# Turning the attention weights by DMA instead of on TensorE in a graph-network kernel

## The chip, the cores and the metric

The kernel runs on one core of one Trainium2 chip. The metric is the time of one execution on the device in microseconds (us); lower is better. A kernel's time is the median over its runs. One execution with a hardware profile stands beside the times.

Five engines work side by side, each on its own list of instructions in a fixed order: TensorE (PE in the profile; PEld is its loading of weights), VectorE (DVE), ScalarE (ACT), GpSimd (POOL) and SyncE (SP), which here only issues DMA transfers. They wait for each other through semaphores. TensorE writes to PSUM; the kernel uses eight banks of 128 x 512 fp32 numbers.

## The reference, cut to what matters

There are 128 graphs of 128 nodes with 256 features; `x` is 128 x 128 x 256 fp32, `adj` a 0/1 matrix for each graph.

```python
# layer 0: three rounds of a gated graph network
h = relu(layernorm(x))
A = (adj != 0)
for i in range(3):
    m = h @ weight[i]
    aggr = einsum('bst,bsd->btd', A, m)           # sum over the edges that come in
    h = gru_cell(aggr, h, w_ih, w_hh, b_ih, b_hh) # gates r, z, n
x = x + h
# layer 1: one graph-attention layer
h = relu(layernorm(x))
Wh = h @ W
s = Wh.sum(-1)
e = leaky_relu(s[:, :, None] + s[:, None, :], 0.2)
e = where(adj == 0, -inf, e)
alpha = softmax(e)                                # over the last axis
x = x + einsum('bpq,bqo->bpo', alpha, Wh)
```

The change concerns the last two lines: the exponentials of `e` (128 x 128 for a graph) are needed with rows and columns exchanged before TensorE can multiply them with `h`.

## The kernel before, in words

**Tiling.** Four graphs make a group (`G = 4`), so there are `NG = 32` groups. A group passes through three rounds of the GRU and then the attention. One round of one group is a *turn*; the list `turns` in the kernel interleaves the 96 turns so that three groups are in flight.

**A turn.** The products of the GRU are arranged as a fast matrix scheme of seven block products (function `products`). They use six PSUM banks: `x_rz`, `x_n`, `y_rz`, `y_n`, `q_rz`, `q_n`. In their order they are X1, Q5, Y6, Y7, X2, Y4, Q3 (the letter is the bank, the number the block product; in the last round, which works on rows, five and seven, three and four are exchanged). Between Y6 and Y7, and between Y7 and Y4, ScalarE copies `y_rz` and `y_n` to SBUF (`put`, L691), and TensorE may not write the bank again before that copy has read it.

**Attention of a group** (function `attention`). The steps are: `normed` writes `h1` (there is one such buffer); VectorE forms the node scores `s`; TensorE spreads `s` over a bank (L891); VectorE adds, applies the leaky relu and takes the row maximum (L885 to L904); ScalarE takes the exponential (L909), with a change of function table before and after; VectorE sums it (L911); TensorE turns the four 128 x 128 tiles of `e` into a bank `misc` (L917); ScalarE copies the bank to `eT` (L919, one buffer); TensorE multiplies `h1` by `eT` in two pieces (`weighted`, L610) and ScalarE copies each to `uT`; TensorE multiplies `uT` by `W` (L930, two pieces); VectorE scales by the inverse sum and adds to `x1` (L935); SyncE stores. The last group does this in two halves.

**The filler banks.** All products on TensorE that are not of the GRU scheme, the edge sums (L596) and the four kinds of attention (L891, L917, L610, L930), take turns in two PSUM banks, both called `misc`.

**DMA transposes that exist already.** Where `h` changes between rows and columns, `turned_halves` (L535 to L539) splits each fp32 number into its two 16-bit halves, which ScalarE writes as two planes (`pl`), turns both planes with one DMA transpose issued by SyncE (L545), and lets ScalarE put the halves together again. One such step covers 128 x 512 numbers, as many as the attention weights of a group.

**What sets the order.** Nothing runs in the order of the source text. Every operation is recorded with an engine, a cost in ns that the author gave, its reads and writes, and a due time (class `Plan`). `Plan.run` then simulates the engines with these costs, and at each step issues on each engine, among the operations that could start first, the one with the most urgent rank. A rank comes from the due time of the operation and of all that depends on it. The GRU products are a fixed chain with due times of one `SLOT` for each turn; what feeds the chain must be ready `MARGIN` ns ahead of it. `plan.due` gives the due time of a group's attention, in slots. The result is a static order for each engine; the costs have no other effect on the program.

Of the kernel before, what the change touches and what calls it, by code (L numbers as in the profile page):

```python
# [16 lines left out]
P = 128  # L17
G = 4
# [2 lines left out]
SETS = 4  # L21
EARLY = 3
SLOT = 18150
MARGIN = 5000
GATES = 18150
BIG = 3.0e38

# [9 lines left out]
class Plan:  # L37
# [28 lines left out]
    def op(self, eng, ns, fn, reads=(), writes=(), room=(), due=None, mark=None,  # L66
           turn=None, two=False, lag=None):

        i, deps = len(self.nodes), set()
        for b in room:
            if b.prev is not None:
                deps.update(a[0] for a in b.prev.accesses)
        for is_write, group in ((False, reads), (True, writes)):
            for item in group:
                b, lo, hi = item if isinstance(item, tuple) else (item, 0, 1 << 30)
                for j, w, l, h in b.accesses:
                    if (w or is_write) and l < hi and lo < h:  # L80
                        deps.add(j)
                if is_write and b.prev is not None:
                    deps.update(a[0] for a in b.prev.accesses)
        for is_write, group in ((False, reads), (True, writes)):
            for item in group:
                b, lo, hi = item if isinstance(item, tuple) else (item, 0, 1 << 30)
                b.accesses.append((i, is_write, lo, hi))
        deps.discard(i)
        bufs = {id(x[0] if isinstance(x, tuple) else x): (x[0] if isinstance(x, tuple) else x)
                for x in list(reads) + list(writes) + list(room)}  # L90
        free = [b for b in bufs.values() if self.tags[b.tag][1] in ("free", "turn")]
        for b in free:
            b.users.append(i)
            b.left += 1
        self.nodes.append([eng, ns, fn, deps, free, self.due if due is None else due,
                           two or eng == "POOL", self.LAG[eng] if lag is None else lag])
        if due is not None:
            self.chain.append(i)
        if mark is not None:
            self.marks[mark] = i  # L100
        if turn is not None:
            self.turns.append((i, turn))
# [108 lines left out]
def kernel(  # L211
# [37 lines left out]
        "at": (1, "all", work, [P, G, N]), "a": (6, "all", work, [P, G, N]),  # L249
        "hT": (1, "set", work, [P, KD, GN]), "rows": (3, "turn", work, [P, G, D]),  # L250
        "pl": (1, "turn", work, [P, 2, 3, GN]), "plT": (1, "turn", work, [P, 2, 3, GN]),
        "r1": (1, "turn", work, [P, G, D]), "p3": (1, "turn", work, [P, G, D]),
        "hs": (2, "turn", work, [P, 4, H]), "aT": (2, "turn", work, [P, KD, GN]),
        "gs": (2, "turn", work, [P, 4, H]),
# [21 lines left out]
        "w1": (1, "all", const, [P, KD, D]), "w1_out": (1, "all", const, [P, KD]),  # L276
        "w1_sum": (1, "all", const, [P, D]),
    }
    DTYPE = {"at": I32, "a": BF16, "pl": U16, "plT": U16, "p3": BF16}
    phys = {}  # L280

    def make(tag, n, kind, pool, shape):
# [191 lines left out]
    def normed(src, dst, lo=0, hi=G):  # L474

        st, mv, rs, nm = buf("st"), buf("mv"), buf("rs"), buf("nm")
        part = slice(lo, hi)
        for b in range(lo, hi):
            op("DVE", 415, lambda b=b: nc.vector.bn_stats(ap(st)[:, b, :], ap(src)[:, b, :]),
               [(src, b, b + 1)], [(st, b, b + 1)])  # L480

        def aggr():
            for b in range(lo, hi):
                nc.vector.bn_aggr(ap(mv)[:, b, :], ap(st)[:, b, :])
        op("DVE", 160 * (hi - lo), aggr, [st], [mv])

        def rstd():
            nc.gpsimd.tensor_tensor(ap(rs)[:, part], ap(mv)[:, part, 1], eps[:, part], OP.add)
            nc.gpsimd.tensor_tensor(ap(rs)[:, part], ap(rs)[:, part], neghalf[:, part], OP.pow)
        op("POOL", 1300, rstd, [mv], [rs])  # L490
        op("DVE", 170, lambda: nc.vector.scalar_tensor_tensor(
            ap(nm)[:, part], ap(mv)[:, part, 0], -1.0, ap(rs)[:, part], op0=OP.mult, op1=OP.mult),
           [mv, rs], [nm])
        for b in range(lo, hi):
            op("ACT", 600, lambda b=b: nc.scalar.activation(
                ap(dst)[:, b, :], ap(src)[:, b, :], AF.Relu, bias=ap(nm)[:, b:b + 1],
                scale=ap(rs)[:, b:b + 1]), [(src, b, b + 1), rs, nm], [(dst, b, b + 1)])

    def flat(b):
        return ap(b).rearrange("p q n -> p (q n)")  # L500
# [26 lines left out]
    def turned_halves(src, rows, dst):  # L527

        pl, plT = buf("pl"), buf("plT")

        def planes(b, k):
            return ap(b)[:, k, 0:2].rearrange("p two (g m) -> p two g m", g=G)
        for k in range(KD):
            units = [src] if rows else [(src, 2 * k, 2 * k + 2)]
            op("ACT", 960, lambda k=k: nc.scalar.copy(  # L535
                planes(pl, k), halves_of(src, rows)[:, k]), units, [(pl, k, k + 1)])
            transpose(pl, plT, k, 2)
            units = [(dst, 2 * k, 2 * k + 2)] if rows else [dst]
            op("ACT", 960, lambda k=k: nc.scalar.copy(  # L539
                halves_of(dst, not rows)[:, k], planes(plT, k)),  # L540
               [(plT, k, k + 1)], units)

# [272 lines left out]
    def phase(g, layer):  # L815
        return turns.index((g, layer))

    def group(g):
        graphs = slice(g * G, (g + 1) * G)
        plan.phase = phase(g, 0)  # L820
        plan.due = (plan.phase - 1) * SLOT
        rows0, at, a, hT = buf("rows"), buf("at"), buf("a"), buf("hT")
        op("SP", 100, lambda: nc.sync.dma_start(ap(rows0), x[graphs].rearrange("b n d -> n b d")),
           [], [rows0])
        op("SP", 100, lambda: nc.sync.dma_start(ap(at), adj[graphs].rearrange("b n m -> n b m")),
           [], [at])
        op("DVE", 420, lambda: nc.vector.tensor_scalar(ap(a), ap(at), 0.0, None,
                                                       op0=OP.not_equal), [at], [a])
        plan.due = (phase(g, L - 1) + 2) * SLOT
        normed(rows0, rows0)  # L830
        for layer in range(L):
            plan.phase = phase(g, layer)
            if layer == 0:
                if g < EARLY:
                    rows_to_T(rows0, hT)
                else:
                    turned_halves(rows0, True, hT)
                parts = parts_of(rows0)
            elif layer < L - 1:
                parts = turned_parts(hT)  # L840
            else:
                rows, x1, h1 = buf("rows"), buf("x1"), buf("h1")
                turned_halves(hT, False, rows)
                parts = parts_of(rows)
                op("SP", 100, lambda: nc.sync.dma_start(
                    ap(x1), x[graphs].rearrange("b n d -> n b d")), [], [x1])
            hs, aT, gs = buf("hs"), buf("aT"), buf("gs")
            node_sums(hT, hs, "POOL", 1390, 940)
            edge_sums(parts, a, aT)
            node_sums(aT, gs, "DVE", 690, 440)  # L850
            plan.cursor = plan.phase * SLOT
            if layer < L - 1:
                gru(layer, hT, hs, aT, gs)
        plan.due = (phase(g, L - 1) + 3) * SLOT
        gru_rows(L - 1, hT, hs, aT, gs, rows, x1)
        for lo, hi in ((0, G),) if g < NG - 1 else ((G // 2, G), (0, G // 2)):
            attention(g, a, x1, h1, lo, hi)

    def attention(g, a, x1, h1, lo, hi):
# [47 lines left out]
        def exps():  # L907
            for b in range(lo, hi):
                nc.scalar.activation(ap(e)[:, b, :], ap(e)[:, b, :], AF.Exp, bias=ap(low)[:, b:b + 1])  # L909
        op("ACT", 2600 + 390 * n, exps, [low], [e], turn=(g + 2, 1, "rz"))  # L910
        op("DVE", cost, lambda: nc.vector.tensor_reduce(small(den), es(), AX.X, OP.add), [e], [den])  # L911
        op("DVE", 170, lambda: nc.vector.reciprocal(small(rden), small(den)), [den], [rden])
        p_e, eT, uT = buf("misc"), buf("eT"), buf("uT")

        def turn():
            for b in range(lo, hi):
                nc.tensor.transpose(flat(p_e)[:, b * N:(b + 1) * N], ap(e)[:, b, :], ident)  # L917
        op("PE", 110 * n, turn, [e], [p_e], [eT])
        op("ACT", 190 + 100 * n, lambda: nc.scalar.copy(  # L919
            ap(eT)[:, part].rearrange("p b n -> p (b n)"), flat(p_e)[:, lo * N:hi * N]),  # L920
           [p_e], [(eT, lo, hi)])

        weighted(h1, eT, uT, lo, hi)
        for m in range(lo, hi, 2):
# [13 lines left out]
        op("SP", 100, lambda: nc.sync.dma_start(  # L938
            out[g * G + lo:g * G + hi].rearrange("b n d -> n b d"), ap(x1)[:, part]),
           [(x1, lo, hi)], [])  # L940

    weights()
    for g in range(NG):
# [33 lines left out]
```

## Time and profile before

| | |
|---|---|
| time, median of 3 runs | 2150.49 us (2149.06 to 2151.18) |
| span of the profiled execution | 2151.8 us |
| PE busy | 2124.3 us, 99% |
| PEld busy | 1894.7 us, 88% |
| DVE busy | 1693.9 us, 79% |
| ACT busy | 1543.7 us, 72% |
| POOL busy | 948.4 us, 44% |
| 16 DMA engines, mean share | 24.9% over three queues |
| DMA transposes | 186, median 3.3 us from issue to landing |

Busy time is the union of an engine's instructions. [...] the cost of a matmul in a stream is the distance from one start to the next, not its duration. In the timeline, neighbouring instructions of one line are merged; "x4" is their number, and an fp32 matmul shows as two records, except the transposes, which show as one.

### The profile page before, as it was taken

To read this page: it belongs to the slowest core of one execution; us is meant where nothing else is said; L and a number is where in the kernel's file an instruction comes from. 1 tells how busy PE (TensorE), PEld (TensorE's weight loads), DVE (VectorE), ACT (ScalarE), POOL (GpSimd) and SP (SyncE) were. 2 spreads that over 40 slices of the span, in tenths; PEclk is the share of its full clock that TensorE was granted. 3 is DMA by queue.
4 is the path that set the end of the run, shared out by engine and by line. 5 is a ranking of instruction groups with operands and counts; after the bars stand their busy time and mean duration, and the time that the engine had idled before them with its cause. 6 is when DMAs were issued, how large, how long until landed. Compare 5 with 4: busy or idle time off the path is not lost.

```text
span 2151.8 us, 34116 instructions
## 1 busy us (share of the span) xinstructions
PE 2124.3 (99%) x12670; PEld 1894.7 (88%) x12670; DVE 1693.9 (79%) x3297; ACT 1543.7 (72%) x2675; POOL 948.4 (44%) x889
## 2 busy tenths in 40 slices
PE   8999999999999999999999999999999999999997
PEld 7888888998889998888998899998899988898885
DVE  5778887887877778777787877878777787877776
ACT  5567877776777777767777777777777778676673
POOL 5645453344544435443445534445534345334331
PEclk9999999999999999999999999999999999999998
DMA  4222122222322222212122223223222213212110
GB/s 142 45 50 50 43 43 64 59 50 50 70 62 57 60 50 50 69 50 69 42 52 65 67 52 62 48 53 66 62 57 60 50 45 69 74 36 49 40 50 30
DMA packets 301750, 121.49 MB, mean 56 GB/s; under 512 B 232976, under 2 KB 301328, under 8 KB 301584
## 3 DMA queue, kind: packets, MB, share of 16 engines
q1 hardware_dynamic: 301584, 119.31, 24.5%
q8 instruction: 99, 1.62, 0.3%
q14 instruction: 67, 0.55, 0.1%
HBM read 45.36 MB, written 16.78 MB: 29 GB/s over the span
## 4 chain that ended last, share of the span: by engine, by line
PE 92%; DVE 5%; DMA 1%; ACT 1%; issue 1%; POOL 0%; DVEq 0%; ACTq 0%; POOLq 0%
PE y_rz L654 14%; PE q_rz L654 10%; PE x_rz L654 10%; PE y_rz L661 8%; PE y_n L654 7%; PE misc L596 6%; PE q_rz L661 5%; PE x_rz L661 5%; PE x_n L654 5%; PE q_n L654 5%; PE misc L930 5%; PE y_n L661 4%; PE x_n L661 3%; PE misc L610 3%; PE q_n L661 3%
## 5 line engine op out<-in xcount | busy, mean ns | idle before, releaser
L624 POOL TENSOR_TENSOR hs<-hT 128x512 f32<-128x512 f32 x96 | 128.8, 1342 | 326.3 <-PE y_n L661 275.9
L556 POOL TENSOR_TENSOR r<-rows 128x512 f32<-128x512 f32 x128 | 146.5, 1163 | 259.8 <-ACT rows L539 170.9
L691 ACT COPY t_rz<-y_rz 128x512 f32<-128x512 f32 x192 | 112.0, 583 | 191.9 <-PE y_rz L654 111.1
L654 PE MATMUL y_rz<-hs,s_hh 128*128 128x256 f32 x768 | 198.6, 381 | 0.2 <-ACT t_rz L691 0.2
L654 PE MATMUL y_rz<-gs,s_x 128*128 128x256 f32 x768 | 197.4, 380 | 0.0
L694 DVE TENSOR_TENSOR t_rz<-t_rz,q_rz 128x512 f32<-128x512 f32 x192 | 131.1, 683 | 70.0 <-ACT t_rz L691 36.5
L654 PEld LDWEIGHTS y_rz<-gs,s_x 128*128 128x128 f32 x768 | 146.4, 191 | 20.0
L654 PEld LDWEIGHTS y_rz<-hs,s_hh 128*128 128x128 f32 x768 | 144.3, 191 | 21.2 <-ACT t_rz L691 1.8
L628 POOL TENSOR_TENSOR hs<-hT,hs 128x256 f32<-128x256 f32 x96 | 75.0, 789 | 196.2 <-PE q_n L661 186.1
L559 POOL TENSOR_TENSOR p<-r 128x512 bf16<-128x512 f32 x128 | 155.5, 1233 | 0.3
L798 POOL TENSOR_TENSOR x<-x,u 128x512 f32<-128x512 f32 x64 | 84.8, 1341 | 157.9 <-DMA x<-in_x_dram 83.6
L691 ACT COPY t_n<-y_n 128x512 f32<-128x512 f32 x192 | 112.4, 585 | 52.3 <-PE y_n L654 20.7
L694 DVE TENSOR_TENSOR t_n<-t_n,q_n 128x512 f32<-128x512 f32 x192 | 131.1, 683 | 23.8 <-ACT t_n L691 9.1
L599 ACT COPY aT<-misc 128x512 f32<-128x512 f32 x192 | 111.7, 584 | 38.0 <-PE misc L596 30.3
L654 PE MATMUL x_rz<-aT,s_x 128*128 128x256 f32 x512 | 131.5, 379 | 0.0
L654 PE MATMUL x_rz<-hT,s_hh 128*128 128x256 f32 x512 | 131.5, 379 | 0.0
L576 POOL TENSOR_TENSOR d<-hT,pl 128x512 f32<-128x512 f32 x64 | 84.1, 1318 | 93.9 <-ACT pl L574 84.1
L930 PE MATMUL misc<-w,uT 128*128 128x256 f32 x512 | 122.8, 384 | 0.3 <-ACT uT L615 0.2
L755 ACT ACTIVATE u<-u,bias_i 128x512 f32<-128x512 f32 x128 | 92.1, 721 | 37.8 <-DVE u L746 37.5
L654 PE MATMUL y_n<-hs,s_hh 128*128 128x256 f32 x384 | 114.5, 380 | 0.3 <-ACT t_n L691 0.2
L654 PE MATMUL y_n<-gs,s_x 128*128 128x256 f32 x384 | 114.3, 379 | 0.0
L763 DVE TENSOR_TENSOR hT<-u,d 128x512 f32<-128x512 f32 x128 | 110.1, 862 | 3.5
(212 smaller groups left out, 6425.7 us busy)
## 6 DMA issues: line engine op xcount, KB each, us to landing
rows<-in_x_dram SPq DMA_DIRECT2D x32, 512.0 KB, 4.3
x<-in_x_dram SPq DMA_DIRECT2D x32, 512.0 KB, 3.9
out_dram<-x SPq DMA_DIRECT2D x31, 512.0 KB, 2.9
at<-in_adj_dram SPq DMA_DIRECT2D x32, 256.0 KB, 2.9
plT<-pl SPq DMA_TRANSPOSE x186, 3.3
rz<-in_L_gnn_w_ih_dram SPq DMA_DIRECT2D x1, 768.0 KB, 5.0
e<-in_L_gnn_weight_dram SPq DMA_DIRECT2D x3, 256.0 KB, 5.6
rz<-in_L_gnn_w_hh_dram SPq DMA_DIRECT2D x1, 768.0 KB, 7.9
```

The costliest lines, as they stand in the source:

```text
L556: op("POOL", 1106, lambda part=part: nc.gpsimd.tensor_tensor(ap(r1)[:, part], ap(rows)[:, part], top(rows)[:, part], OP.subtract), [(rows, ...
L559: op("POOL", 1050, lambda part=part: nc.gpsimd.tensor_tensor(ap(p3)[:, part], ap(r1)[:, part], top(r1)[:, part], OP.subtract), [(r1, n, n ...
L596: nc.tensor.matmul(flat(ps)[:, b * N:(b + 1) * N], part(i, b, k), ap(a)[:, b, :], start=(i == 0), stop=(i == 2))
L599: op("ACT", 590, lambda k=k, ps=ps: nc.scalar.copy(ap(dst)[:, k, :], flat(ps)), [ps], [(dst, 2 * k, 2 * k + 2)])
L624: op(eng, cost, lambda: sub(ap(w)[:, 0:2, :], blocks()[:, 1::2, :], blocks()[:, 0:2, :], OP.subtract), [t], [(w, 0, 2)], two=True)
L654: nc.tensor.matmul(ap(bank)[:, half, :], ap(w)[:, i - 1, q, :], source(t, sums), start=(first and c == 0 and m == 0), stop=False, skip_gro ...
L661: nc.tensor.matmul(ap(bank)[:, m, half * P:(half + len(chunk)) * P], source(t, sums)[:, m * N:(m + 1) * N], ap(w)[:, i - 1, q:q + len(chun ...
L691: op("ACT", 590, lambda: nc.scalar.copy(ap(t), ap(y)), [y], [t])
L694: op("DVE", 690, lambda: nc.vector.tensor_tensor(ap(t), ap(t), ap(q), OP.add), [q], [t])
L755: op("ACT", 723, lambda j=j, cols=cols: nc.scalar.activation(ap(u)[:, cols], ap(u)[:, cols], AF.Tanh, bias=ap(W["bias_i"])[:, 2 * KD + j:2 ...
L763: op("DVE", 690, lambda j=j, d=d, cols=cols: nc.vector.tensor_tensor(ap(hT)[:, j, :], ap(u)[:, cols], ap(d), OP.add), [(u, lo, hi), d], [( ...
L930: nc.tensor.matmul(ap(ps)[:, b, :], ap(uT)[:, k, (m + b) * N:(m + b + 1) * N], ap(w1)[:, k, :], start=(k == 0), stop=(k == KD - 1))
```

## The change

The four transposes on TensorE, and the copy from their bank, are replaced for 30 of the 32 groups. ScalarE now splits `e` into 16-bit halves (`pe`), one DMA transpose turns both planes (`peT`), and ScalarE interleaves the halves again into `eT`. This frees TensorE of the transposes and frees the `misc` bank they used. The last two groups keep the old way. The scheduler gets a larger `MARGIN`, other costs for several ScalarE operations, and a due time for the attention of the last groups that is no later than half a slot after the last turn.

```diff
-MARGIN = 5000
+MARGIN = 8000
...
+        "pe": (1, "all", work, [P, 2, G * N]), "peT": (1, "all", work, [P, 2, G * N]),
...
-            op("ACT", 600, lambda b=b: nc.scalar.activation(
+            op("ACT", 520, lambda b=b: nc.scalar.activation(
...
-            op("ACT", 960, lambda k=k: nc.scalar.copy(
+            op("ACT", 1045, lambda k=k: nc.scalar.copy(
                 planes(pl, k), halves_of(src, rows)[:, k]), units, [(pl, k, k + 1)])
...
-            op("ACT", 960, lambda k=k: nc.scalar.copy(
+            op("ACT", 1340, lambda k=k: nc.scalar.copy(
                 halves_of(dst, not rows)[:, k], planes(plT, k)),
...
-        plan.due = (phase(g, L - 1) + 3) * SLOT
+        plan.due = min(phase(g, L - 1) + 3, len(turns) + 0.5) * SLOT
...
-        op("ACT", 2600 + 390 * n, exps, [low], [e], turn=(g + 2, 1, "rz"))
+        op("ACT", 2570 * (g < NG - 1) + 320 * n, exps, [low], [e], turn=(g + 2, 1, "rz"))
...
-        p_e, eT, uT = buf("misc"), buf("eT"), buf("uT")
-
-        def turn():
-            for b in range(lo, hi):
-                nc.tensor.transpose(flat(p_e)[:, b * N:(b + 1) * N], ap(e)[:, b, :], ident)
-        op("PE", 110 * n, turn, [e], [p_e], [eT])
-        op("ACT", 190 + 100 * n, lambda: nc.scalar.copy(
-            ap(eT)[:, part].rearrange("p b n -> p (b n)"), flat(p_e)[:, lo * N:hi * N]),
-           [p_e], [(eT, lo, hi)])
+        eT, uT = buf("eT"), buf("uT")
+        if g < NG - 2:
+            turned_weights(e, eT)
+        else:
+            p_e = buf("misc")
...
...
+    def turned_weights(e, eT):
+        pe, peT = buf("pe"), buf("peT")
+        def halves(t):
+            return ap(t).rearrange("p g n -> p (g n)").bitcast(U16).rearrange(
+                "p (m two) -> p two m", two=2)
+        op("ACT", 1045, lambda: nc.scalar.copy(ap(pe), halves(e)), [e], [pe])
+        op("SP", 100, lambda: nc.sync.dma_start_transpose(
+            ap(peT).rearrange("p two (g q) -> p (two g) q", q=P),
+            ap(pe).rearrange("p two m -> p (two m)")), [pe], [peT])
+        op("ACT", 1340, lambda: nc.scalar.copy(halves(eT), ap(peT)), [peT], [eT])
```

More of the change, by code (lines that the diff above doesn't have):

```diff
@@ L278 @@
     }
-    DTYPE = {"at": I32, "a": BF16, "pl": U16, "plT": U16, "p3": BF16}
+    DTYPE = {"at": I32, "a": BF16, "pl": U16, "plT": U16, "pe": U16, "peT": U16, "p3": BF16}
     phys = {}
@@ L909, in exps, with turn @@
                 nc.scalar.activation(ap(e)[:, b, :], ap(e)[:, b, :], AF.Exp, bias=ap(low)[:, b:b + 1])
-        op("ACT", 2600 + 390 * n, exps, [low], [e], turn=(g + 2, 1, "rz"))
+        op("ACT", 2570 * (g < NG - 1) + 320 * n, exps, [low], [e], turn=(g + 2, 1, "rz"))
         op("DVE", cost, lambda: nc.vector.tensor_reduce(small(den), es(), AX.X, OP.add), [e], [den])
         op("DVE", 170, lambda: nc.vector.reciprocal(small(rden), small(den)), [den], [rden])
-        p_e, eT, uT = buf("misc"), buf("eT"), buf("uT")
-        def turn():
-            for b in range(lo, hi):
-                nc.tensor.transpose(flat(p_e)[:, b * N:(b + 1) * N], ap(e)[:, b, :], ident)
-        op("PE", 110 * n, turn, [e], [p_e], [eT])
-        op("ACT", 190 + 100 * n, lambda: nc.scalar.copy(
-            ap(eT)[:, part].rearrange("p b n -> p (b n)"), flat(p_e)[:, lo * N:hi * N]),
-           [p_e], [(eT, lo, hi)])
+        eT, uT = buf("eT"), buf("uT")
[3 more added lines that the diff above has]
+            p_e = buf("misc")
+            def turn():
+                for b in range(lo, hi):
+                    nc.tensor.transpose(flat(p_e)[:, b * N:(b + 1) * N], ap(e)[:, b, :], ident)
+            op("PE", 110 * n, turn, [e], [p_e], [eT])
+            op("ACT", 190 + 100 * n, lambda: nc.scalar.copy(
+                ap(eT)[:, part].rearrange("p b n -> p (b n)"), flat(p_e)[:, lo * N:hi * N]),
+               [p_e], [(eT, lo, hi)])
         weighted(h1, eT, uT, lo, hi)
```

## The prediction

> **What bounds the kernel now.** I read the page's busy shares and slices first, then the waits of TensorE, then its timeline in a middle stretch and at the end.
>
> ```profile
> PE 2124.3 (99%) x12670; PEld 1894.7 (88%) x12670; DVE 1693.9 (79%) x3297; ACT 1543.7 (72%) x2675; POOL 948.4 (44%) x889
> PE   8999999999999999999999999999999999999997
> PEclk9999999999999999999999999999999999999998
> ```
>
> TensorE is full in every slice but the first and the last. Busy could still hide stretched matmuls, so I checked the waits from 110 to 2000 us (first three lines) and 2000 to 2112 us (last two):
>
> ```profile
> PE misc L610 <- ACT aT L599: 2.6, 2, 1.6
> PE y_n L654 <- ACT t_n L691: 0.2, 1, 0.2
> PE y_rz L654 <- ACT t_rz L691: 0.2, 1, 0.2
> PE q_rz L661 <- DVE gs L624: 1.8, 1, 1.8
> PE misc L610 <- ACT eT L919: 0.4, 1, 0.4
> ```
>
> That is 5.2 us of waiting in 2000 us. So in the middle any work taken off TensorE is time taken off the kernel, and any work added on another engine is free until TensorE waits for it. The removed transposes stand in this stream:
>
> ```profile
> 1025.93 0.59 PE L654 MATMUL y_n<-gs,s_x 128*128 128x256 f32 x2
> 1026.37 0.60 PE L917 MATMUL misc<-ident,e 128*128 128x128 f32 x4
> 1026.80 1.03 PE L654 MATMUL y_rz<-hs,s_hh 128*128 128x256 f32 x4
> ```
>
> The columns are start, length, and instruction. The four transposes last 0.60 us, but from their start to the next start is 0.43 us; that is their price. They stand between Y6 (ends with y_n) and Y7 (starts with y_rz). The end is different:
>
> ```profile
> 2109.57 3.62 PE L930 MATMUL misc<-w,uT 128*128 128x256 f32 x16
> 2115.64 0.72 PE L891 MATMUL misc<-ident,s 128*128 128x128 f32 x3
> 2116.59 0.32 PE L891 MATMUL misc<-ident,s 128*128 128x128 f32 x1 [0.22 <-DVE hw L867]
> 2121.12 1.35 PE L917 MATMUL misc<-ident,e 128*128 128x128 f32 x4 [4.21 <-ACT e L909]
> ```
>
> The last GRU product has been issued at 2115.64 us. From there to the end, 36.2 us, the attention of the last two groups runs with TensorE waiting, and the chain of waits names VectorE for most of 2117 to 2136 us. The L930 products at 2109.57 us stood ahead of that point, on the full engine.
>
> **What the Trainium skill says.** *VectorE: DVE Perf Modes*, "The three transpose paths", gives a 128x128 bf16 transpose 390 ns on TensorE (into PSUM) and 1309 ns by DMA (into SBUF). In the stream here four fp32 ones cost 0.43 us, so 108 ns each; the DMA ones land 3.3 us after issue. The DMA way is slower, then, and pays only because TensorE is the full engine. *DMA: Bandwidth & Descriptors*, "DMA Transpose (X-bar)", admits 2-byte types only, which is why ScalarE must split and join; the existing copies around such transposes measure 1046 and 1338 ns. *ScalarE: Activation LUTs*, "What ACT_TABLE_LOAD costs", gives 1283 ns for a load; the trace has 31 before the exponentials, mean 1283 ns. *TensorE: Matmul & The Clock Gate*, part 1, says an idle array drops to half clock for some microseconds. The trace agrees: after 2120 us the clock is 0.66 to 0.78 and L930 starts lie 0.43 us apart, against 0.22 us before.
>
> **The change part by part.**
>
> *Removed from TensorE.* 30 groups x 0.43 us (timeline above; the spread is small, all have one form) = 12.9 to 13.1 us. I take **13.1**, four times 109.5 ns a group.
>
> *ScalarE.* Added per group: one split of 1.05 us and one join of 1.34 us, the same 128x1024 16-bit forms as L535 and L539. Removed: the copy from the bank, 0.59 us. 30 x (1.05 + 1.34 - 0.59) = 54 us, so 1544 becomes about 1598 us, 75% of a span of 2136. It lies beside the full TensorE: **0**, as long as no copy of Y (L691) comes late behind a 1.34 us join.
>
> *DMA.* 30 transposes join 186, of the same size, each some 1.3 us of SyncE's issue time; the DMA engines go from 25% to perhaps 28%. The chain from exponential to L610 grows from about 1 us (transposes, copy) to 1.05 + 3.3 + 1.34 plus hand-overs, some 6.5 us. Behind the waiting DMA on SyncE stand loads for later turns and other transposes; behind the waiting join on ScalarE stand copies of Y, for which TensorE does wait. The bounds come from the landings of the transposes in the trace, 3.0 to 5.4 us. The plan prices the new one at 4.1 us (100 ns and the usual lag of 4000). The 122 joins that exist waited 0.2 us in all for their DMA. In the new program's order 25 us or more of TensorE work lie between L891 of a group and its first L610 (51 to 56 us before), for score additions 3, exponential with tables 4 to 5, and the 6.5: enough. I take **1 us** lost over the 30 groups; bounds 0 and 8 (a quarter of a microsecond each, if half of the late landings reach ScalarE at a bad moment).
>
> *Fillers.* Between Y6 and Y7 TensorE has to give ScalarE time for the copy. In the old order 5 of 96 such places had nothing between, in the new one 8; 49 have an L610 piece and 27 an L930 piece where L917 or L891 stood. In the trace of before the empty places cost 0.2 us each at most. **0**, bounds 0 and 2.
>
> *New costs and margin.* They change no instruction. They bring the plan to the durations in the trace: 520 for the relu (2.07 us for four), 1045 and 1340, 2570 for two tables and 320 an exponential (1.28 us for four). The named waits of 4.9 us in mid-kernel may go or come elsewhere: **0**, bounds -3 and +3.
>
> *Start.* The new order loads `x` and `w_hh` ahead of the first message weight (which landed at 6.45 us; the fourth transfer landed at 10.24). The first composed weights come later, but what ended TensorE's start was VectorE's gs at 28.6 us (a wait of 3.4 us). Walking the new VectorE order with the old durations, gs comes at about 27, and four small transposes already stand inside the wait. **1 us gained**, bounds -2 and +3.
>
> *End.* With the common due time both L930 pieces of group 29 move behind the last GRU product: one ahead of L891 of group 30, one after it. Counting the order with the start-to-start prices, work up to the last product falls from 2082.1 to 2065.5 us: 16.6 = 13.1 + 3.5. The 3.5 us move into the wait of 4.2 us. It isn't all gain. L891 comes 1.7 us after the last product instead of at once, so the score chain (3.1 us on VectorE) starts about 0.9 us later; the four L935 of group 29 (0.42 us each) now stand in the VectorE chain ahead of the next normalisation, partly under GpSimd's 1.0 us there; and L917 of group 30 must wait for its bank until the first L935 pair has read it. I make the tail 1.5 to 2.5 us longer: **1.5 gained** net, bounds -1 and +3.5.
>
> Sum: 13.1 - 1 + 0 + 0 + 1 + 1.5 = 14.6; 2150.5 - 14.6 = **2136 us**.
>
> **The rivals.**
>
> *A. The DMA becomes a wait on ScalarE.* Landing at 5.4 instead of 3.3 us leaves ScalarE standing for about 1.5 us, and copies of Y behind it come late; 0.25 us for each of 30 groups on TensorE is 7.5 us: 2143.5. For: ScalarE's order is static and goes to 75%. Against: 122 such joins wait 0.2 us in all now.
>
> *B. Start and end give their full bound.* 13.1 + 3.5 + 3 = 19.6: 2131. For: VectorE was late with L935 and hw just before the last products, and gets free there. Against: the VectorE chain of the end is only reordered.
>
> *C. Slower.* If every transpose is late by its whole spread (2.1 us), and half reaches TensorE, 30 x 1.05 = 31 us against 14.6 gained: 2167; with 0.6 us each, 2154. For: one `eT`, one `pe`, one `h1`, so a late group holds up the next one's scores. Against: 25 us less 3, 4.5 and 6.5 leaves some 11 us of slack in that chain.
>
> *D. No change*, 2150: the filler places left bare cost as much as the transposes did, 0.44 us at each of 30. Against: at the places that are bare now, 0.2 us at most.
>
> **How the numbers follow.** Forecast 0.71, A 0.12, B 0.09, C 0.05, D 0.03. Predicted is 2136. B lies at the lower edge and A at the upper one: 2130.5 to 2143 leaves out C, D and the outer parts of A and B, about 0.17 in all. Faster by over 0.2% (under 2146.2) takes in the forecast, A and B, 0.92; same 0.03; slower 0.05.
>
> **What would show each step.** TensorE busy falls by some 13 us with 120 fewer matmuls; L917 is left with 8 of 128. The waits of TensorE between 110 and 2090 us stay under 8 us, none on L610 from the new join. ScalarE's joins wait for DMA a few us in all; rival A shows there as 20 us and more, with Y products waiting for L691. The last GRU product comes about 16 to 18 us earlier than 2115.6, with L930 right behind it; the tail after it is 37 to 39 us. The first gs product comes near 27 us. The forecast is wrong if TensorE's summed waits grow by more than 7 us, or the tail by more than 5.

## The result and the profile after

The changed kernel takes 2140.14 us (median of 6 runs, 2138.75 to 2141.19) against 2150.78 us (6 runs, 2148.45 to 2151.4). The ratio is 0.9952, 95% interval 0.9939 to 0.9965: 10.3 us less, between 7.5 and 13.1. The forecast of 2136 was 4 us too low; the time lies in the stated range.

The page of the changed kernel, its busy line and TensorE's slices:

```profile
PE 2108.1 (99%) x12550; PEld 1879.9 (88%) x12550; DVE 1750.7 (82%) x3297; ACT 1587.1 (74%) x2705; POOL 951.0 (45%) x889
...
PE   8999999999999999999999999999999999999997
```

TensorE runs 120 matmuls fewer and is as full as before; its busy time fell by 16.2 us in this pair. ScalarE is busy 43 us longer, 1587.1 against 1543.7 us. Lines of the changed kernel are numbered 1 to 5 higher than in the kernel before: L654, L691, L917, L930 and L935 there are L655, L692, L922, L935 and L940 here (in the experiments up to 3 higher still). Two groups of instructions, the transposes that are left and the new join (busy, mean ns of one, idle time before and what ended it):

```profile
L922 PE MATMUL misc<-ident,e 128*128 128x128 f32 x8 | 2.2, 398 | 5.6 <-DVE x L940 5.6
```

```profile
L958 ACT COPY eT<-peT 128x1024 uint16<-128x1024 uint16 x30 | 40.4, 1347 | 1.9 <-DMA peT<-pe 1.9
```

The join waits 1.9 us in all for its DMA: the DMA is not late. But the eight transposes that stay on TensorE now wait 5.6 us. The waits of TensorE from 110 to 2100 us (each line: us in total, times, longest in us):

```profile
PE y_rz L655 <- ACT t_rz L692: 2.6, 3, 1.4
PE y_rz L662 <- ACT t_rz L692: 1.4, 1, 1.4
PE x_rz L662 <- ACT x_rz L687: 1.2, 1, 1.2
PE misc L935 <- DVE x L940: 1.0, 1, 1.0
PE misc L597 <- ACT uT L616: 0.8, 1, 0.8
PE misc L597 <- DMA plT<-pl: 0.2, 1, 0.2
```

That is 7.2 us where 5.2 stood before, mostly in new places, and none is a wait of L611 for the join. The waits for ScalarE's copies of Y (L692) make 4.0 of it, against 0.4 before. TensorE's timeline at the end (each line: start, length, engine, line of code; in brackets the wait before it and what ended it):

```profile
2099.71 1.89 PE L935 MATMUL misc<-w,uT 128*128 128x256 f32 x8
2101.44 0.60 PE L892 MATMUL misc<-ident,s 128*128 128x128 f32 x4
2102.95 1.99 PE L935 MATMUL misc<-w,uT 128*128 128x256 f32 x8 [0.92 <-DVE e L898]
2110.08 1.08 PE L922 MATMUL misc<-ident,e 128*128 128x128 f32 x4 [5.13 <-DVE x L940]
```

The last GRU product has been issued by 2099.71 us, 15.9 us earlier than in the first trace of before; in the second traces of both kernels the distance is 11.1 us (2101.44 against 2112.49). The two L935 pieces of group 29 stand behind it as the new order has them. Then comes a wait of 5.1 us: L922 needs the filler bank that the first L935 filled, and VectorE empties that bank only after the GRU work of group 31.

**Where the time went.** For each trace I split the span in four: the work up to the last GRU product at its start-to-start price, which is the usual distance from one matmul's start to the next of its form (0.22 us for an fp32 128x256 one, which lasts 0.38 us in the profile); what TensorE's starts lost on that price in the first 110 us; what they lost from there to the last product; and the end after it (1.4 us before the first matmul are left out). Two traces each of before and after, one of the others:

| kernel | work | lost, start | lost, middle | end | span |
|---|---|---|---|---|---|
| before | 2081.8 | 14.9 / 13.8 | 17.5 / 15.5 | 36.2 / 34.9 | 2151.8 / 2147.4 |
| after | 2065.3 | 13.1 / 14.3 | 19.9 / 20.4 | 37.2 / 37.3 | 2136.9 / 2138.8 |
| DMA turn alone | 2068.7 | 14.4 | 19.9 | 34.4 | 2138.8 |
| scheduler alone | 2078.3 | 13.6 | 16.6 | 37.6 | 2147.6 |
| old due times | 2068.7 | 14.5 | 19.9 | 33.9 | 2138.4 |
| old margin | 2065.7 | 8.0 | 28.8 | 34.2 | 2138.0 |
| transposes doubled | 2094.9 | 14.9 | 14.3 | 34.7 | 2160.2 |
| own bank at the end | 2065.3 | 13.2 | 20.0 | 32.8 | 2132.7 |

Means of after against before: work -16.5, start -0.7, middle +3.6, end +1.7, sum -11.9. The first pair of traces alone lies 14.9 us apart; the first trace of before was a long one, 4.4 us over the second in start, middle and end together, so it is the timed runs that give the size.

### The profile page after: what moved, and what is told of

Its sections match the earlier page's. It is cut to its first block, busy times and chain, and to the rows that moved or that the text cites. A ratio compares the mean times of both kernels' runs of the same rounds, so it can differ in the third digit from the quotient of the medians.

```text
span 2136.9 us, 33989 instructions
## 1 busy us (share of the span) xinstructions
PE 2108.1 (99%) x12550; PEld 1879.9 (88%) x12550; DVE 1750.7 (82%) x3297; ACT 1587.1 (74%) x2705; POOL 951.0 (45%) x889
## 4 chain that ended last, share of the span: by engine, by line
PE 94%; DVE 3%; ACT 1%; DMA 1%; issue 1%; SPq 0%; DVEq 0%; ACTq 0%
PE y_rz L655 15%; PE q_rz L655 10%; PE x_rz L655 10%; PE y_rz L662 8%; PE y_n L655 7%; PE misc L597 6%; PE q_rz L662 5%; PE x_n L655 5%; PE x_rz L662 5%; PE q_n L655 5%; PE misc L935 5%; PE y_n L662 4%; PE misc L611 3%; PE x_n L662 3%; PE q_n L662 3%; PE misc L892 1%
## 5 line engine op out<-in xcount | busy, mean ns | idle before, releaser
L692 ACT COPY t_rz<-y_rz 128x512 f32<-128x512 f32 x192 | 112.3, 585 | 200.5 <-PE y_rz L662 104.9
L625 POOL TENSOR_TENSOR hs<-hT 128x512 f32<-128x512 f32 x96 | 131.3, 1368 | 183.7 <-PE y_n L662 126.7
L655 PE MATMUL y_rz<-hs,s_hh 128*128 128x256 f32 x768 | 198.0, 380 | 2.6 <-ACT t_rz L692 2.6
L655 PE MATMUL y_rz<-gs,s_x 128*128 128x256 f32 x768 | 197.1, 379 | 0.0
L582 POOL TENSOR_TENSOR pl<-d,pl 128x512 bf16<-128x512 f32 x64 | 77.9, 1219 | 217.8 <-ACT pl L580 217.7
L560 POOL TENSOR_TENSOR p<-r 128x512 bf16<-128x512 f32 x128 | 168.1, 1332 | 0.0
L655 PEld LDWEIGHTS y_rz<-gs,s_x 128*128 128x128 f32 x768 | 146.0, 190 | 19.8
L655 PEld LDWEIGHTS y_rz<-hs,s_hh 128*128 128x128 f32 x768 | 141.5, 190 | 21.8 <-ACT t_rz L692 4.0
L577 POOL TENSOR_TENSOR d<-hT,pl 128x512 f32<-128x512 f32 x64 | 77.9, 1221 | 131.6 <-ACT pl L575 125.9
L692 ACT COPY t_n<-y_n 128x512 f32<-128x512 f32 x192 | 112.1, 584 | 29.5 <-PE y_n L655 16.8
L655 PE MATMUL x_rz<-hT,s_hh 128*128 128x256 f32 x512 | 131.5, 379 | 0.0
L655 PE MATMUL x_rz<-aT,s_x 128*128 128x256 f32 x512 | 131.5, 379 | 0.0
L935 PE MATMUL misc<-w,uT 128*128 128x256 f32 x512 | 121.7, 383 | 3.1 <-DVE e L898 1.7
L625 DVE TENSOR_TENSOR gs<-aT 128x512 f32<-128x512 f32 x96 | 96.8, 1009 | 27.4 <-ACT aT L600 27.4
L759 DVE TENSOR_TENSOR d<-hT,u 128x512 f32<-128x512 f32 x128 | 106.0, 828 | 12.2 <-ACT u L756 12.1
L655 PE MATMUL y_n<-hs,s_hh 128*128 128x256 f32 x384 | 114.5, 380 | 0.0
```

Of the source, the lines that this page charges most:

```text
L560: op("POOL", 1050, lambda part=part: nc.gpsimd.tensor_tensor(ap(p3)[:, part], ap(r1)[:, part], top(r1)[:, part], OP.subtract), [(r1, n, n ...
L625: op(eng, cost, lambda: sub(ap(w)[:, 0:2, :], blocks()[:, 1::2, :], blocks()[:, 0:2, :], OP.subtract), [t], [(w, 0, 2)], two=True)
L655: nc.tensor.matmul(ap(bank)[:, half, :], ap(w)[:, i - 1, q, :], source(t, sums), start=(first and c == 0 and m == 0), stop=False, skip_gro ...
L692: op("ACT", 590, lambda: nc.scalar.copy(ap(t), ap(y)), [y], [t])
L759: op("DVE", 690, lambda j=j, d=d, cols=cols: nc.vector.tensor_tensor(ap(d), ap(hT)[:, j, :], ap(u)[:, cols], OP.subtract), [(hT, lo, hi), ...
L935: nc.tensor.matmul(ap(ps)[:, b, :], ap(uT)[:, k, (m + b) * N:(m + b + 1) * N], ap(w1)[:, k, :], start=(k == 0), stop=(k == KD - 1))
```

## The experiments

All ratios are to the kernel before on the same chip, with 95% intervals. The unaltered kernels were run again for a second trace.

> The changed kernel unaltered, for a second trace and a tighter ratio beside the kernels below. Theory 1 (TensorE is full, 13 us of transposes are gone, the rest is small): 2136 to 2140, ratio 0.9935 to 0.9955. Its trace shows how far the profiled pair (14.9 us apart) was chance: if the start and the named waits in mid-kernel differ from the first trace by some us, the pair overstated the gain.

Measured: 2140.64 us, ratio 0.9953 (0.9940 to 0.9965), inside the expected ratios. The two traces of the changed kernel differ by 1.2 us at the start and 0.5 in the middle.

> The kernel before unaltered, for a second trace. Its first profiled execution was 3 us over the median of its timed ones. Theory: the waits of mid-kernel (6.5 us in places over 120 ns) and the order are the same, and what varies is the half clock of the start (14.5 us lost in the first 40 us) and of the end (36.2 us after the last GRU product), by 1 to 2 us each. Rival: the mid-kernel waits are what varies, by 3 us or more.

Measured: 2149.16 us, ratio 0.9998 (0.9989 to 1.0007). Between the two traces of before the start differs by 1.1 us, the middle by 2.0 and the end by 1.3. Start and end vary as the theory says, but the middle, which it took to be steady, varies most, though not by the rival's 3 us.

**The two halves of the change.** The scheduler's part without the DMA, and then the reverse, the DMA with the old margin, costs and due times. The edit of the first:

```diff
-        if g < NG - 2:
+        if g < 0:
```

> The changed kernel with the transposes of all 32 groups back on TensorE; margin, costs and common due time stay new. Work up to the last GRU product 2078.6 us by start-to-start prices (before 2082.1, after 2065.5). Theory 1: only the end and the start are left, 2147 to 2150, at most 3 us under before. Rival 2 (the gain is the scheduler's, the transposes were free fillers): 2140 to 2142.

Measured: 2148.99 us, ratio 0.9994 (0.9986 to 1.0002): no gain that can be measured.

> The kernel before with the DMA turning for 30 groups alone; margin, costs and due times are the old ones. Work up to the last GRU product 2068.9 us. Theory 1: 13 us less than before, 2136 to 2139, if the old costs don't bring new waits of TensorE. Rival 2: 2148 to 2151. Rival A (the DMA is late and ScalarE stands): over 2143, with joins waiting 20 us and more.

Measured: 2138.56 us, ratio 0.9944 (0.9930 to 0.9958). The DMA turn alone has the whole gain, 12.0 us (9.0 to 15.1). Rival 2, that the gain is the scheduler's, falls. The interval overlaps that of the whole change.

**The price of a transpose on TensorE.** The kernel before issues its four transposes twice:

```diff
-            for b in range(lo, hi):
+            for b in list(range(lo, hi)) * (2 if g < NG - 2 else 1):
                 nc.tensor.transpose(flat(p_e)[:, b * N:(b + 1) * N], ap(e)[:, b, :], ident)
```

> The kernel before with the four transposes issued twice, into the same places, in 30 groups; the order of all else is unchanged. Theory 1: 30 x 0.43 = 13 us more than before, 2163 to 2164. Rival 2 and rival D (as fillers they cost nothing): 2150 to 2154.

Measured: 2160.24 us, ratio 1.0046 (1.0033 to 1.0058), 9.9 us more (7.1 to 12.5), which lies between the two expectations. The work grew by 13.1 us, but the middle lost 14.3 us where before lost 15.5 to 17.5: the longer fillers seem to have covered 1 to 3 us of other waits, though the two traces of before differ by 2.0 there. With the transposes gone the middle goes the other way, from 16.5 to 20.1 us in the mean. So four transposes are worth 0.43 us in the stream; to the kernel they were worth about 0.33 us when added, and 0.40 us when the DMA turn alone took them away (12.0 us over 30 groups).

**How near the DMA is to being late.** The DMA transpose is issued twice into the same buffer; the order on every engine stays. The second one waits on SyncE until the first has landed, so a join's data come 3.1 us later (median), the far end of the 1.2 to 3 us that I had written.

```diff
+            for _ in range(2):
                 nc.sync.dma_start_transpose(
                     ap(peT)..., ap(pe)...)
```

> The changed kernel with the new DMA transpose issued twice, one after the other, in all 30 groups; the order of all else is unchanged. Each join then gets its data 1.2 us (one issue) to 3 us later. Theory 1 (slack hides the DMA): ScalarE's joins wait 20 to 40 us in all, TensorE's summed waits grow by no more than 3 us, 2140 to 2143. Rival A (a late join holds up copies of Y): 8 us or more on top, 2148 and over.

Measured: 2180.43 us, ratio 1.0142 (1.0127 to 1.0158), some 41 us over the changed kernel. My theory that slack hides such a delay was badly wrong, and rival A's mechanism appears once the delay is there. ScalarE's waits and TensorE's in this kernel:

```profile
ACT eT L961 <- DMA peT<-pe: 58.4, 27, 4.0
...
ACT rows L540 <- DMA plT<-pl: 10.2, 11, 1.8
```

```profile
PE misc L597 <- DMA plT<-pl: 12.8, 4, 3.6
PE y_rz L655 <- ACT t_rz L692: 10.4, 11, 2.7
...
PE q_rz L655 <- DVE t_rz L695: 5.4, 5, 2.2
```

ScalarE's timeline around one join, first of the changed kernel, then of this one:

```profile
862.91 0.60 ACT L778 ACTIVATE rz<-y_rz 128x512 f32<-128x512 f32 x1 [1.26 <-PE y_rz L662]
864.33 1.35 ACT L958 COPY eT<-peT 128x1024 uint16<-128x1024 uint16 x1 [0.82 <-DMA peT<-pe]
865.55 0.62 ACT L795 ACTIVATE u<-u 128x512 f32<-128x512 f32 x1
```

```profile
476.33 0.60 ACT L778 ACTIVATE rz<-y_rz 128x512 f32<-128x512 f32 x1 [1.26 <-PE y_rz L662]
479.46 1.34 ACT L961 COPY eT<-peT 128x1024 uint16<-128x1024 uint16 x1 [2.54 <-DMA peT<-pe]
480.67 0.62 ACT L795 ACTIVATE u<-u 128x512 f32<-128x512 f32 x1
```

The join stands in the middle of the GRU's work on ScalarE, right where the plan thinks that the data come. In the changed kernel the median join begins 0.65 us after its landing, and 16 of 30 under 1 us. Add 3.1 us, and ScalarE's new joins stand for 56 us more, and TensorE's middle loses 42 us more (62.0 us by the table's reckoning, against 19.9 and 20.4).

Is it the place of the join or the second transpose itself? The plan is told a longer delay for it; the two transposes stay:

```diff
-        op("SP", 100, turn_twice, [pe], [peT])
+        op("SP", 100, turn_twice, [pe], [peT], lag=7500)
```

> The kernel with the new DMA transpose issued twice, whose 3.1 us of added delay cost 40 us, with one change to the plan: it now reckons 7.6 us from issue to landing in place of 4.1, so that ScalarE's order places the join later. The DMA work is the same. Theory 4 (the delay was dear because ScalarE's fixed order has a join stand right behind its transfer, so ScalarE and then TensorE stand still): the loss falls from 40 us to under 6, 2139 to 2146, and joins wait under 6 us in all. Rival (the second transpose itself is dear: the DMA engines, the issue queue, or the single buffer that holds up the next group): 2165 to 2182.

Measured: 2155.30 us, ratio 1.0026 (1.0016 to 1.0036). The new joins wait 3.2 us, yet 15.9 of the 41 us stay. The place of the join explains about 25 us, the second transpose itself the rest, and neither expected number was met. The waits of ScalarE, and one of SyncE's queue, show where the rest is:

```profile
ACT rows L540 <- DMA plT<-pl: 32.9, 17, 3.3
...
ACT hT L540 <- DMA plT<-pl: 3.5, 3, 2.3
```

```profile
SPq L957 <- DMA peT<-pe: 65.1, 30, 3.4
```

SyncE stands 65 us for the first transpose to land, in order, and the GRU's own transposes wait behind it; their joins wait 36 us for them, 2 us in the changed kernel. Whether other waits play a part too was not tried, and the longer delay in the plan also shifts other operations.

**Due time and margin.** One line each is set back:

```diff
-        plan.due = min(phase(g, L - 1) + 3, len(turns) + 0.5) * SLOT
+        plan.due = (phase(g, L - 1) + 3) * SLOT
```

> The changed kernel with the old due times of the last groups' attention; all else new. Both L935 products of group 29 stand ahead of the last GRU product again (2068.9 us of work up to it, 12.2 after). Theory of the prediction: the common due time is worth 1.5 us, so 2141.5 to 2142.5 here. Rival 3 (it moves 3.5 us of work behind the last product and pays them back in the wait for the bank): 2138 to 2140.5, no different from the changed kernel or faster.

Measured: 2138.38 us, ratio 0.9950 (0.9938 to 0.9963), the same as with the new due time. The 1.5 us that I had put on it are not there; rival 3 is. In the table, the new due time takes 3.4 us of work from ahead of the last product and adds 3.3 us to the end.

```diff
-MARGIN = 8000
+MARGIN = 5000
```

> The changed kernel with the old margin of 5000; this also brings back the old order of the first loads (message weight ahead of x and w_hh). Theory of the prediction: the margin itself is worth nothing and the new order of the first loads about 1 us, so 0 to 2 us slower than the changed kernel, ratio to before 0.9950 to 0.9965. Rival: the larger margin guards TensorE from late feeds, and without it the waits of mid-kernel grow by 3 us and more, ratio over 0.997. Rival: it costs, and the ratio is under 0.9945.

Measured: 2140.78 us, ratio 0.9966 (0.9952 to 0.9979), which overlaps the changed kernel's interval and lies between the theory's range and the rival's. The trace is more telling than the time. The start loses 8.0 us in place of 13 to 14. The old order of the first loads is not enough to explain that, since before and the DMA turn alone have it too and lose 13.8 to 14.9. What differs in the trace is that gs comes at 26.59 us (28.15 to 28.74 in those and in the changed kernel) and that the granted clock from 26 to 34 us is 1.00, against 0.57 to 0.79 in the others; why is open. And the middle loses 28.8 us in place of 20, for one line above all:

```profile
PE y_rz L655 <- ACT t_rz L692: 7.5, 2, 4.9
```

Two trades of 5 to 9 us almost cancel. With one trace of this kernel, their sizes are rough.

**A version that beats both.** In the changed kernel, only the bank of the last transposes is another: `q_rz`, which is idle after the last turn.

```diff
-            p_e = buf("misc")
+            now, plan.phase = plan.phase, len(turns) + g + (lo == 0)
+            p_e = buf("q_rz")
+            plan.phase = now
```

> The changed kernel with the PE transposes of the last two groups written to the bank q_rz, which is idle after the last turn, instead of a shared filler bank. In the changed kernel they waited 5.1 us for VectorE to empty their bank. Theory 1 (the new order of the end made this wait, and the chain passes through it): the time after the last GRU product falls from 37.2 to 33 to 35 us, in all 2136 to 2138.5. Rival: VectorE's chain bounds the end anyway, under 1 us of gain, 2139.5 to 2141.

Measured: 2134.68 us, ratio 0.9929 (0.9917 to 0.9942), better than expected and 15.3 us under before; by the ratios some 5 us under the changed kernel, though the intervals just touch. The end falls from 37.2 to 32.8 us:

```profile
2103.15 1.99 PE L937 MATMUL misc<-w,uT 128*128 128x256 f32 x8 [0.92 <-DVE e L898]
2105.96 1.21 PE L924 MATMUL q_rz<-ident,e 128*128 128x128 f32 x4 [0.82 <-ACT e L910]
2110.28 3.75 PE L611 MATMUL misc<-eT,h 128*128 128x128 f32 x16 [3.11 <-DVE x L942]
```

The transposes (L924) start 4.1 us earlier, as soon as the exponentials are there. What is left is the same wait for a bank, one step later. Giving L611 idle banks too, and then also more slack for the join (`lag=5500`):

> The changed kernel with three idle GRU banks for the attention of the last two groups: q_rz for the transposes, q_n and x_n for the two L611 pieces. With q_rz alone the time was 2134.7, and a wait of 3.1 us of the first L611 piece for a filler bank was left. If the end is bound by banks: 1 to 3 us less, 2131.5 to 2134. If VectorE's chain takes over: 2134 to 2135.5.

Measured: 2135.85 us, ratio 0.9937 (0.9923 to 0.9950), above both expected ranges; no further gain. L611 starts 2.7 us earlier (2107.55 us), yet the end is 33.4 us. In the trace VectorE works without a listed wait from 2097.7 to 2120.2 us, which fits the expectation that its chain takes over.

> The kernel with three idle banks, and the plan reckons 5.6 us from issue to landing of the new transpose, not 4.1. If late landings (up to 5.1 us) cost the changed kernel TensorE time: the joins' 2 us of waits go, and 1 to 2 us of time with them, 2130 to 2133. If they cost nothing, or the later join makes its own waits: the same as with three banks alone, or 1 us more.

Measured: 2137.31 us, ratio 0.9942 (0.9929 to 0.9954). The joins wait 0.0 us now (median 3.5 us after landing), and the time is not better. That doesn't clear the 2 us of joins' waits in the changed kernel: by the table's reckoning the middle loses 22.2 us here against 19.8 with three banks alone, since the later plan makes waits of its own, for copies of Y above all.

## Why the prediction was right, point by point

Term by term, the forecast was 13.1 removed, 1 lost at the joins, 0 for fillers and costs, 1 gained at the start and 1.5 at the end: 14.6. The traces have 13.1, 3.6 lost in the middle, 0.7 and 1.7 gained: 11.9. The timed runs have 10.3. Most of the signs that the forecast named came: waits of 7.2 us (under 8), joins waiting 1.9 us, a tail of 37.2 us, eight transposes left.

**The bound: right.** TensorE stayed full, and work taken off it came off the time. The DMA turn alone has the gain, the scheduler's part alone none that can be measured.

**13.1 us removed: right in the stream, somewhat less in the kernel.** Doubling the transposes added 9.9 us, not 13.1, and the DMA turn alone took away 12.0; the interval of the second still holds 13.1.

**ScalarE, 54 us: right as a sum of durations.** The durations grew by 56.0 us. Busy time grew by only 43, because neighbouring instructions overlap in the profile: the join at 864.33 us above lasts 1.35 us, and the next instruction starts at 865.55.

**Fillers at 0 and joins at -1: the mis-sized term.** Together with the new costs, also at 0, they say that the middle loses 1 us; it lost 3.6 in the mean of the traces, inside the bounds that I gave but 2.6 us over their sum. Four of the 7.2 us of named waits are for late copies of Y, the road of rival A. But the new joins are not what stands in front there. ScalarE ahead of one of the two longest of these waits (1.35 us, it ends at 227.59 us), in the changed kernel:

```profile
222.07 2.53 ACT L540 COPY rows<-plT 128x1024 uint16<-128x1024 uint16 x2
224.63 1.28 ACT L778 ACT_TABLE_LOAD   x1
225.92 0.63 ACT L778 ACTIVATE rz<-t_rz 128x512 f32<-128x512 f32 x1
226.46 0.61 ACT L795 ACTIVATE u<-u 128x512 f32<-128x512 f32 x1
226.98 0.56 ACT L692 COPY t_rz<-y_rz 128x512 f32<-128x512 f32 x1
227.44 1.04 ACT L954 COPY pe<-e 128x1024 uint16<-128x1024 uint16 x1
```

The copy comes behind GRU work that was there before, and the split stands after it. At none of the six places where TensorE waits for ScalarE in this trace is a new split or join among the three ScalarE instructions ahead of the one waited for. The second trace has the Y waits at the same instructions, the scheduler alone has two of them (0.92 and 1.47 us), so they come from the fixed order and not from chance. What makes the order with the DMA lose more was not separated, the added work on ScalarE or the missing fillers: every kernel with the DMA turn and the new margin or the old costs loses 19.9 to 20.4 us there, every one with single transposes on TensorE 15.5 to 17.5. With one trace of most kernels, differences under 2 us there say nothing.

**"25 us or more of TensorE work ... enough": the wrong room, without effect by luck of the lag.** I counted the room between L891 and L610 on TensorE, and TensorE indeed never waited for the join there. The room that counts is on ScalarE, between landing and join, and it is 0.65 us in the median. The landings stayed at 3.0 to 5.1 us (median 3.2), as they had to for the bound of 8 us, and the plan's 4.1 us just held; with 3.1 us more at every group the place of the join cost about 25 us, and the doubled DMA 41 us in all.

**Start, +1: a wash.** gs came at 28.38 us, against 28.62, not at 27; the start lost 0.7 us less in the mean, which is less than its own scatter. In the old margin's trace gs does come near 27 us, and 5 to 6 us less are lost, so there was more to gain at the start than the new plan got.

**End, +1.5: not there in the direct test.** Against before, work -3.4 and end +1.7 give 1.7 us, which looks right. But the run that sets only the due time back has the same time (0.9950 against 0.9952), and its end, 33.9 us, is 1.7 us shorter than before's mean. So the sum for the end came out by luck, and not by the due time. The steps named were right, the wait of L917 (L922 in the new kernel) for its bank above all, but I gave it no number; it is 5.1 us. Against the old due time, the end gives back 3.3 of the 3.4 us that leave the work. One reading of before needs a limit: after 2120 us the half rate, 0.43 us from start to start, holds for the eight L930 at 2140.21 us; the fourteen at 2127.61 us still stand 0.22 us apart.

**Rivals.** B and D did not come. C did not come, and of A only the late copies of Y, at 4.0 us and not behind the joins. But the doubled DMA is rival C in size: the road is there, with less than 1 us of room ahead of 16 of the 30 joins.

## What to carry to other kernels

If one engine is full, moving work to a slower path can gain even when that path takes far longer (here 0.43 us in TensorE's stream against a landing of 3.2 us and a split and a join on ScalarE), but look at what the removed work was covering: here 13.1 us went and the middle lost 3.6 us more than before. The slack of a transfer is not the room ahead of its last user; it is the room ahead of the first instruction that waits for it in a fixed order. When that room is used up, everything queued behind the instruction waits too, on its engine and on the queue that issues. Where the end of a program waits for a buffer, look for one that the main loop has left idle.

## What the runs showed of the hardware that was not expected

VectorE became 56 us busier (1694 to 1750 us, in two traces each) with the same 3297 instructions. The one on a 128x512 fp32 sum (L625) lasts 683 to 693 ns in the changed kernel when no GpSimd instruction runs beside it; when one does, 678 to 1606 ns, 1193 on average. 61 of 96 have one beside them there, 47 of 96 before, where these lasted 829 ns on average. So a GpSimd instruction beside it does not slow it always, and what decides was not tried; POOL's own spans are rough in the profile. With the old margin VectorE is at 1699 us and the time is no better, but that kernel differs in more than this, so whether it costs time is not shown.
